# The input products of steps 4 to 7 of a residual LSTM: plain products replaced by two units of a seven-product scheme

## The chip, the core and the metric

The kernel runs on one core of one Trainium2 chip. The metric is the device time of one execution, in microseconds; where several runs stand together, their median is given. A core has five engines that each take their own instructions strictly in the order in which the program lists them: TensorE (PE in the profile; PEld is its weight loads), VectorE (DVE), ScalarE (ACT), GpSimd (POOL) and SyncE (SP). Here SyncE only issues transfers, and the others meet through semaphores.

## The reference, cut to what matters

An LSTM runs over 512 steps for 32 sequences with 512 inputs and 512 hidden units, in float32, and its outputs are added to its inputs.

```python
def lstm_forward(x, h0, Wx, Wh, b):           # x: 32 x 512 x 512, Wx and Wh: 512 x 2048
    xW = jnp.einsum('ntd,dg->ntg', x, Wx) + b # all steps, no recurrence
    def step(carry, xw_t):
        prev_h, prev_c = carry
        a = xw_t + prev_h @ Wh
        i, f, o = (sigmoid(a[:, k * Hd:(k + 1) * Hd]) for k in range(3))
        g = jnp.tanh(a[:, 3 * Hd:])
        next_c = f * prev_c + i * g
        return (o * jnp.tanh(next_c), next_c), o * jnp.tanh(next_c)
    ...
return x + lstm_forward(x, cond_1024, Wx, Wh, b)
```

`prev_h @ Wh` must be done step by step. `xW` has no recurrence, so its products can be done ahead and with fewer multiplications.

## The kernel before, in words

**Tiling.** A matmul of the kernel has 128 rows of contraction, 32 stationary columns (the 32 sequences of one step, or 32 rows of the state) and 256, 384, 128 or 512 moving columns. Four such matmuls, one for each quarter of the array's columns, run beside each other. Eight steps of `x` make a row (`ROW`); row 0 holds steps 0 to 7. The gate columns are cut in four blocks `j` of 512 (`NJ`), and the contraction in four quarters `q`. The weights `Wx` lie in SBUF as eight tiles `raw_sb`/`raw[i]`.

**Three ways to the input products.** (1) Plain (`direct`): 16 matmuls of 512 columns for a step. (2) A one-level unit: a 2 by 2 block scheme with seven products in place of eight, for one row and one block `j`. Its left sides are blocks of `x` or sums of them (`inner_sums`, the tiles `s_h`), its right sides are weights or differences of weights (`t_sums`, the tiles `t`). A unit needs seven product groups; each is eight matmuls of 256 columns, four for either half `k` of the contraction. (3) From row 4 on, two-level schemes (`PAIR`, `CYCLE`) whose right sides, the factors, are made once by VectorE (`push_factors`, tiles `wa_make` and `wb_make`), written to DRAM (`keep`) and streamed back.

**Windows.** Everything of ways 2 and 3 is paced by windows `v`. A unit that begins in window `v` has product group 1 and 5 in `v`, 6 in `v+1`, 7 in `v+2`, 2 and 3 in `v+3`, 4 in `v+4` (`products`). Between the windows' groups other engines must work (`evacuate`): ScalarE copies the accumulator `acc` after group 1 (`pu`) and group 5's bank `p`; VectorE adds `acc` and the copy of `p` after group 6 (into `pu`, called the pu add below: L617 before, L619 after) and again after group 7 (into `pp`, the pp add: L624 before, L626 after). Group 7 is added into the same half of `acc` that the pu add reads, so it waits for that add. One tile `acc` is one PSUM bank with two halves, and unit `n+2` has the other half of unit `n`'s tile; the program lets group 6 of unit `n+2` wait for the pp add of unit `n`.

**Order.** The program is written in one order by hand; each engine runs its share of it. VectorE's factor work is queued in `due` and let in by `run_due` within a room of columns: up to 1200 at a window's start, up to 1300 before the pp add, and up to 2400 more in a window that lies ahead of step 0. The operations of a window stand on VectorE's queue in just that order, so a pu add or pp add stands behind the factor work let in ahead of it.

**Ahead of step 0.** Steps 0 to 3 are done plainly while the weights arrive, into the four banks `firsts`, and kept by VectorE with the bias (`keep_direct`). Then window 0 (unit (1, 0)) and windows 1 to 4: each has one plain step (4 to 7) into a bank of `gates` and, up to window 3, the groups of the units of row 1. The first `PAIR_ROW - 1` rows after row 0 are done by units (`UNITS`), one a window. From step 0 on, step `k` runs with window `k + NJ`: 32 matmuls of the state (`h_part`, L851), the window's groups, and the cell.

**After a unit.** ScalarE copies its two result tiles, SyncE stores them to DRAM (`store`), and a later GpSimd transfer that adds (`load_xw`) brings a step's part into `xw`, which ScalarE has filled with the bias (`fill_bias`). Steps 0 to 7 take their `xw` straight from `keep_direct` instead.

Of the kernel before, what the change touches and what calls it, by code (L numbers as in the profile page):

```python
# [9 lines left out]
F32 = mybir.dt.float32  # L10
# [4 lines left out]
P = 128  # L15
B = 32
T = 512
NJ = 4
G = 4
IFG = 3 * P  # L20
ROW = 8
NROWS = T // ROW
C = 256
# [40 lines left out]
SLACK = [2, 2, 2, 8]  # L64
PAIR_SLACK = [2, 6]
AHEAD = 5
FACTORS_TO = 15

RAW_FIRST = 4

# [15 lines left out]

ROWS_AT = rows_by_use()
PAIR_ROW = 4
UNITS = [(i, j) for i in range(1, PAIR_ROW) for j in range(NJ)]

# [68 lines left out]


PAIR_STEP = 9
PAIR_AT = PAIR_STEP + NJ
PAIRS = len(PAIR_A_OF)
START = PAIR_AT + PAIRS
START_STEP = HEAD - LEAD
# [3 lines left out]
def windows_of(k):  # L171

    if k < PAIR_STEP:
        return [k + NJ]
    if k >= START_STEP:
        return [k + OFF]
    steps = START_STEP - PAIR_STEP
    lo, hi = (PAIRS * (k + e - PAIR_STEP) // steps for e in (0, 1))
    return list(range(PAIR_AT + lo, PAIR_AT + hi))
# [102 lines left out]
def kernel(  # L282
# [281 lines left out]
    def product(job, s, part=None):  # L564
        dst = {
            1: job.acc,
            6: job.acc,
            7: job.acc,
            5: p5[:, 0],
            2: job.pp[0][:, 0],  # L570
            3: job.pp[0][:, 1],
            4: job.pp[1][:, 0],
        }[s]
        for m, (a, w) in enumerate(job.factors(s)):
            if part not in (None, m):
                continue
            for t in range(4):
                nc.tensor.matmul(  # L578
                    dst[t * B : (t + 1) * B],
                    a[:, t],  # L580
                    w,
                    start=s in (1, 5) and m == 0,
                    stop=True,
                    skip_group_check=True,
                )
# [55 lines left out]
    def store(i, j, f):  # L641
# [3 lines left out]
        for t in range(4):  # L645
            nc.sync.dma_start(out=to[t, j * B : (j + 1) * B], in_=f[t * B : (t + 1) * B])

    def finish_unit(job, i, j, pool=unit_free):
        def finish(half):
            if half == 0:  # L650
                job.f = pool.pop(0)
            nc.scalar.copy(job.f[:, half], job.pp[half].rearrange("p n c -> p (n c)"))
            if half:
                store(i, j, job.f)
                pool.append(job.f)
            return 0

        return finish
# [113 lines left out]
    def keep_direct(t, bank, room=None):  # L772
        if room is not None:
            xw[t] = room
        elif t < 4:
            xw[t] = upool.tile([P, G * P], F32, name=f"xw_{t}", tag="xw", bufs=4)
        else:
            xw[t] = node_free[t - 4].rearrange("p t e b -> p (t e b)")
        nc.vector.tensor_add(xw[t], flat(bank), bias_sb)  # L779

    pieces = [(t, q, e) for t in range(LATE_END, T) for q in range(NJ) for e in (slice(0, C), slice(C, 2 * C))]
# [189 lines left out]
    for w, j in zip(LATE_AT, LATE_ORDER):  # L971
        job = new_job(w, True)
        job.kind = (None, j)
        job.acc, job.pp = jobs[LATE_AT[0]].acc, jobs[LATE_AT[0]].pp
    head_sums = {}

    def prepare(v):

        job = jobs.get(v)
        ops = []  # L980
        if job is None or job.w >= PAIR_AT:
            return ops
        i, j = job.kind
        for k in range(2):
            if (i, k) not in head_sums:
                if (i, 0) not in head_sums:
                    both = spool.tile([P, 2, 4, 4, B], F32, name=f"s_h{i}", tag="sums", bufs=2)
                head_sums[i, k], more = inner_sums(block(raw_block(i, k)), both[:, k])
                ops += more
        job.factors = lambda s: [  # L990
            (left(block(raw_block(i, k)), s, head_sums[i, k]), raw_factor(NJ * k + j, s)) for k in range(2)
        ]
        job.finish = finish_unit(job, i, j)
        job.release = lambda: None
        return ops
# [78 lines left out]
    def fetch(v):  # L1074

        job = jobs.get(v + 2)
        if job and LATE_AT[0] > job.w >= PAIR_AT and job.kept:
            job.ring = [rpool.tile([P, 3, C], F32, name=f"wa_{job.w}", tag="wa", bufs=3), None]
            nc.sync.dma_start(out=job.ring[0].rearrange("p n c -> p (n c)"), in_=job.kept[0])
        job = jobs.get(v)  # L1080
        if job and LATE_AT[0] > job.w >= PAIR_AT and job.kept:
            job.ring[1] = rpool.tile([P, 4, C], F32, name=f"wb_{job.w}", tag="wb", bufs=4)
            nc.sync.dma_start(out=job.ring[1].rearrange("p n c -> p (n c)"), in_=job.kept[1])
        if v in (LAST - 4, LAST - 2):
            load_row(END // ROW + (v - LAST + 4) // 2)
        for i in [i for i in range(8) if i not in RESIDENT][2 * (v - LAST) - 2 : 2 * (v - LAST)] if v > LAST else ():
            if i in again:
                f = free.pop(0)
                raw[i] = f.rearrange("p h (n c) -> p (h n) c", c=C)
            else:  # L1090
                raw[i] = rpool.tile([P, 4, C], F32, name=f"raw_again_{i}", tag="wb", bufs=4)
            nc.sync.dma_start(out=raw[i].rearrange("p n c -> p (n c)"), in_=wx[i])
        sb, rest = divmod(v + 8 - START, PER)
        if v + 6 in UNIT_AT[2 * NJ :: NJ]:
            load_row(3 + UNIT_AT[2 * NJ :: NJ].index(v + 6))
        if v in (NJ, NJ + 1):
            load_row(PAIR_ROW + v - NJ)
        if rest < MO and 0 <= sb < NSB:
            load_row(HEAD // ROW + MO * sb + ROWS_AT[rest])

    with tc.manual_schedule():
        warm = work.tile([P, G, P], F32, name="warm", tag="s")
        nc.scalar.activation(warm[:, 0], c_init, AF.Sigmoid)
        for m in range(10):
            nc.tensor.matmul(
                pps[2][m % NJ * B : (m % NJ + 1) * B].rearrange("p n c -> p (n c)"),
                c_init[:, 0:B],
                c_init.unsqueeze(1).to_broadcast([P, 4, P]),
                start=True,
                stop=True,  # L1110
            )
        nc.vector.transpose(
            bias_sb.rearrange("p (m l) -> p m l", l=B),
            bias_t.unsqueeze(2).to_broadcast([P, G * NJ, B]),
        )
        firsts = [gates[0], gates[1], pps[0], pps[1]]
        for q in range(4):
            for n in range(2):
                for t in range(4):
                    direct(t, firsts[t], (q,), slice(n * C, (n + 1) * C))  # L1120
        for i in range(5):
            for op in t_sums(i):
                op()
        keep_direct(0, firsts[0])
        for op in prepare(0):
            op()
        products(0)
        for t in range(1, 4):
            keep_direct(t, firsts[t])
        for i in range(5, 8):  # L1130
            for op in t_sums(i):
                op()
        push_factors()
        for v, t in enumerate(range(4, ROW), 1):
            direct(t, gates[t % 2])
            for op in prepare(v):
                op()
            if v < 4:
                evacuate(v, 0)
            run_due(0, 2400 if v > 1 else 0)  # L1140
            keep_direct(t, gates[t % 2])
            if v < 4:
                products(v)
                fetch(v)
        node_free[:] = node_free[NJ:] + node_free[:NJ]
        seed_first(0)
        seed_last(0)
        seed_first(1)

        for k in range(T):  # L1150
            if k % 2 == 0 and k + 2 < T:
                load_residual(k + 2)
            if 5 <= k and k + 3 < LATE_END:
                load_xw(k + 3)
            (h_part if k < HALVES else h_halves)(k)
            for m, v in enumerate(windows_of(k)):
                if v == PAIR_AT + RAW_FIRST - 1:
                    assert factors_left[-1] == 0
                if v == PAIR_AT + 4:
                    head_done()  # L1160
                announce(v)
                room = HEAD_ROOM if v < START - 4 else ROOM if k < HALVES - 1 else HALF_ROOM
                run_due(v, room - evacuate(v, room))
                products(v)
                tail_products(v)
                fetch(v)
                if m == 0:
                    if k == T - 2:
                        x_last()
                    if NJ <= k and k + 4 < LATE_END:  # L1170
                        fill_bias(k + 4)
                    (cell if k < HALVES else cell_halves)(k)
                    seed_first(k + 2)
                    seed_last(k + 1)
                for op in prepare(v + 1):
                    op()
        assert not due
# [51 lines left out]
```

## Time and profile before

| what | value |
|---|---|
| median of 3 runs (lowest to highest) | 3080.84 us (3080.80 to 3081.36) |
| the profiled execution's own time | 3080.69 us |
| its span, first to last instruction | 3078.9 us |
| TensorE busy | 3071.3 us |
| VectorE, ScalarE, GpSimd busy | 2284.0, 1975.9, 808.2 us |
| moved by DMA | 706.25 MB |

The span is what lies between the first and the last instruction; 1.79 us of the execution's own time lie outside it. Times in the timeline are counted from the span's start. In the records a matmul of this kernel stands as two, so a product group of eight stands as a row of x16. A row of the timeline gives start and duration; the duration of a pipelined instruction reaches into the next, so what one instruction costs its engine is read from start to start. Step 0's state products begin at 46.9 us.

### The profile page before, as it was taken

What the parts mean: (1) busy time and instruction counts of PE and PEld (TensorE: products, weight loads), DVE (VectorE), ACT (ScalarE), POOL (GpSimd) and SP (SyncE); (2) the same over time, 40 slices, a digit from 0 to 9 for tenths busy, and PEclk for the clock granted to TensorE, in tenths of its full rate; (3) what the DMA queues carried; (4) which work ended last, traced back from release to release, by engine and by line L of the source; (5) the groups of instructions that cost most, each with busy time, mean ns of one, the idle gap of its engine ahead of it and who ended that gap; (6) DMA issues with size and microseconds to landing.
All of it is one profiled execution on the core that took longest, in us unless ns stands there. A gap on an engine that the chain in (4) does not pass through costs nothing.

```text
span 3078.9 us, 133769 instructions
## 1 busy us (share of the span) xinstructions
PE 3071.3 (100%) x56644; PEld 1980.1 (64%) x56644; DVE 2284.0 (74%) x6437; ACT 1975.9 (64%) x5708; POOL 808.2 (26%) x1009
## 2 busy tenths in 40 slices
PE   9999999999999999999999999999999999999999
PEld 5555555556666666666666666666666666666666
DVE  6766777777777777777777777777777777777754
ACT  2566666666666666666666666766666666666664
POOL 0122222222222222222222222222222222222321
PEclk9999999999999999999999999999999999999999
DMA  9898898888889888898988988889898898988751
GB/s 318 239 260 214 228 258 220 250 224 239 245 212 263 229 239 239 213 265 211 259 224 216 265 224 249 226 222 261 215 261 227 227 255 218 258 226 222 194 118 41
DMA packets 349431, 706.25 MB, mean 229 GB/s; under 512 B 45600, under 2 KB 118688, under 8 KB 348320
## 3 DMA queue, kind: packets, MB, share of 16 engines
q1 hardware_dynamic: 276976, 567.36, 56.0%
q0 software_dynamic: 71424, 130.06, 26.4%
q8 instruction: 446, 7.31, 1.0%
q14 instruction: 153, 1.25, 0.1%
q10 hardware_dynamic: 432, 0.27, 0.0%
HBM read 512.83 MB, written 184.68 MB: 227 GB/s over the span
## 4 chain that ended last, share of the span: by engine, by line
PE 99%; DMA 0%; DVE 0%; ACT 0%; issue 0%; SPq 0%; DVEq 0%
PE gates L851 53%; PE acc L578 17%; PE pp L578 17%; PE p L578 6%; PE gates L865 4%; PE gates L763 1%; PE pp L763 1%; PE acc L763 0%; DMA raw_sb<-in_L_cond_Wx_dram 0%; ACT s L910 0%; DVE fc L916 0%; DVE c L918 0%; DVE fc L922 0%; DVE ig L917 0%; ACT ig L931 0%
## 5 line engine op out<-in xcount | busy, mean ns | idle before, releaser
L851 PE MATMUL gates<-wh_sb,ht 128*32 128x384 f32 (+1 forms) x30144 | 1723.1, 379 | 0.0
L851 PEld LDWEIGHTS gates<-wh_sb,ht 128*32 128x32 f32 x30144 | 1022.7, 110 | 704.5 <-issue 624.0
L954 POOL TENSOR_TENSOR oc<-xr,ht 128x128 f32<-128x128 f32 x509 | 386.3, 759 | 2232.2 <-DVE ht L896 2041.5
L813 POOL DMA_DIRECT2D xw<-xw x496 | 437.0, 881 | 21.4 <-ACT ig L931 2.4
L888 ACT ACTIVATE s<-gates 128x256 f32<-128x256 f32 x472 | 182.3, 386 | 343.4 <-PE gates L851 332.7
L809 ACT COPY xw<-bias_sb 128x512 f32<-128x512 f32 x496 | 313.4, 632 | 0.0
L578 PE MATMUL pp<-wb,nodes 128*32 128x256 f32 x3920 | 312.3, 379 | 0.0
L891 DVE TENSOR_TENSOR fc<-s,c 128x128 f32<-128x128 f32 x471 | 136.8, 290 | 184.4 <-ACT s L888 181.7
L622 ACT COPY pp<-pu 128x512 f32<-128x512 f32 x394 | 237.1, 602 | 53.0 <-DVE t L721 25.9
L895 DVE TENSOR_TENSOR fc<-s,ig 128x128 f32<-128x128 f32 x472 | 137.9, 292 | 177.3 <-ACT ig L894 177.3
L624 DVE TENSOR_TENSOR pp<-acc,p 128x256 f32<-128x256 f32 x394 | 168.4, 427 | 118.2 <-ACT pp L623 118.2
L890 ACT ACTIVATE s<-gates 128x128 f32<-128x128 f32 x472 | 131.4, 278 | 146.9 <-PE gates L851 146.7
L836 ACT COPY gates<-xw 128x384 f32<-128x384 f32 x468 | 221.2, 473 | 5.3 <-DVE nodes L779 5.3
L578 PE MATMUL acc<-wb,s 128*32 128x256 f32 x2656 | 211.5, 379 | 0.0
L578 PE MATMUL pp<-wb,s 128*32 128x256 f32 x2656 | 211.5, 379 | 0.0
L578 PE MATMUL acc<-wa,s 128*32 128x256 f32 x2656 | 211.5, 379 | 0.0
L578 PE MATMUL p<-wa,s 128*32 128x256 f32 x2656 | 211.4, 379 | 0.0
L894 ACT ACTIVATE ig<-c 128x128 f32<-128x128 f32 x472 | 146.3, 310 | 100.9 <-DVE c L893 62.8
L623 ACT COPY pp<-acc 128x256 f32<-128x256 f32 x394 | 142.2, 361 | 90.9 <-DVE t L721 41.1
L617 DVE TENSOR_TENSOR pu<-acc,p 128x256 f32<-128x256 f32 x394 | 163.8, 416 | 44.2 <-ACT p L614 35.4
L896 DVE STREAM_TRANSPOSE ht<-fc 128x128 f32<-128x128 f32 x472 | 147.0, 311 | 50.4 <-DVE fc L895 1.4
L614 ACT COPY p<-p 128x256 f32<-128x256 f32 x394 | 149.6, 380 | 39.8 <-PE p L578 37.7
(224 smaller groups left out, 4493.2 us busy)
## 6 DMA issues: line engine op xcount, KB each, us to landing
wb<-keep_b SPq DMA_DIRECT2D x332, 512.0 KB, 6.2
wa<-keep_a SPq DMA_DIRECT2D x332, 384.0 KB, 5.3
xw<-xw POOLq DMA_DIRECT2D x496, 256.0 KB, 5.7
xw<-t SPq DMA_DIRECT2D x420, 128.0 KB, 3.9
xw<-raw_sb SPq DMA_DIRECT2D x264, 128.0 KB, 3.9
xr<-in_x_dram SPq DMA_DIRECT2D x256, 128.0 KB, 5.5
out_dram<-oc SPq DMA_DIRECT2D x255, 128.0 KB, 4.6
row<-in_x_dram SPq DMA_DIRECT2D x63, 512.0 KB, 8.3
```

Source lines behind the costliest of these rows:

```text
L578: nc.tensor.matmul(dst[t * B : (t + 1) * B], a[:, t], w, start=s in (1, 5) and m == 0, stop=True, skip_group_check=True,)
L614: nc.scalar.copy(job.p5, p5[:, 0])
L617: nc.vector.tensor_add(job.pu[:, 1], job.acc, job.p5)
L622: nc.scalar.copy(job.pp[0], job.pu)
L624: nc.vector.tensor_add(job.pp[1][:, 1], job.acc, job.p5)
L809: nc.scalar.copy(xw[t], bias_sb)
L813: nc.gpsimd.dma_start(out=xw[t], in_=stored[i][a], accum_op=mybir.AluOpType.add)
L836: nc.scalar.copy(gates[t % 2][:, 0:IFG], xw[t][:, 0:IFG])
L851: nc.tensor.matmul(g[j * B : (j + 1) * B, cols], state["ht"][:, k, :], wh_sb[:, k, j, cols], start=False, stop=True, skip_group_check=True,)
L888: nc.scalar.activation(s[:, 0:2], g[:, 0:2], AF.Sigmoid)
L896: nc.vector.transpose(ht.rearrange("p q b -> p (q b)"), h)
L954: (nc.gpsimd if t < T - 3 else nc.vector).tensor_add(state["oc"][:, tt % 2], xr[t][:, tt % 2], ht)
```

## The change

Steps 4 to 7 are no longer done plainly. Two units are put ahead of the others: each has the four steps 4 to 7 (half a row, `h = 1`) and two column blocks, `js = (0, 1)` and `(2, 3)`, where a unit of the other kind has eight steps and one column block. Its groups have as many matmuls as those of the others; the left sides have 64 columns for each half of the contraction in place of 128, and both new units share one set of left sums, kept in a tile of `nodes`. Six units (two new, four of row 1) now stand in windows 0 to 5, ahead of step 0, one after the other; step `k` runs with window `k + 6`, so it meets the same unit as before. The results of steps 4 to 7 go through DRAM as those of later steps do. One weight tile's differences (`t_sums(5)`) are made ahead of window 0 and not behind it. `FACTORS_TO`, the window by which all factors must be made, goes from 15 to 17.

```diff
-FACTORS_TO = 15
+FACTORS_TO = 17
...
-UNITS = [(i, j) for i in range(1, PAIR_ROW) for j in range(NJ)]
+UNITS = [(0, (1, (0, 1))), (0, (1, (2, 3)))] + [(i, j) for i in range(1, PAIR_ROW) for j in range(NJ)]
+FIRST = 2 + NJ
...
-                    a[:, t],
-                    w,
+                    a[:, t % a.shape[1]],
+                    w[t // a.shape[1]] if isinstance(w, list) else w,
...
+    def half_block(src, h):
+
+        return lambda g, e: src[:, 4 * h + 2 * g : 4 * h + 2 * g + 2, e]
+
+    def half_factors(i, h, js, made):
+        return lambda s: [
+            (left(half_block(raw_block(i, k), h), s, made[k]), [raw_factor(NJ * k + j, s) for j in js])
+            for k in range(2)
+        ]
...
-        for i in range(5):
+        for i in range(6):
             for op in t_sums(i):
                 op()
         keep_direct(0, firsts[0])
         for op in prepare(0):
             op()
         products(0)
         for t in range(1, 4):
             keep_direct(t, firsts[t])
-        for i in range(5, 8):
+        for i in range(6, 8):
             for op in t_sums(i):
                 op()
         push_factors()
-        for v, t in enumerate(range(4, ROW), 1):
-            direct(t, gates[t % 2])
+        for v in range(1, FIRST):
             for op in prepare(v):
                 op()
-            if v < 4:
-                evacuate(v, 0)
+            evacuate(v, 0)
             run_due(0, 2400 if v > 1 else 0)
-            keep_direct(t, gates[t % 2])
-            if v < 4:
-                products(v)
-                fetch(v)
-        node_free[:] = node_free[NJ:] + node_free[:NJ]
+            products(v)
+            fetch(v)
+        for op in prepare(FIRST):
+            op()
+        run_due(0, 2400)
...
-            if 5 <= k and k + 3 < LATE_END:
+            if 1 <= k and k + 3 < LATE_END:
                 load_xw(k + 3)
...
-                    if NJ <= k and k + 4 < LATE_END:
+                    if k + 4 < LATE_END:
                         fill_bias(k + 4)
```

Three places show how the instructions move. First TensorE, from group 5 of the second unit to group 1 of the third (`p` is group 5's bank, `acc` the accumulators, `s_h` and `nodes` the left sums). Before:

```order
L578 MATMUL p_85<-t_95,s_h_341 32x256 x4
L578 MATMUL p_85<-t_99,s_h_341 32x256 x4
L763 MATMUL gates_82<-raw_sb,row_102 32x512 x16
L578 MATMUL acc_83<-t_94,s_h_341 32x256 x4
L578 MATMUL acc_83<-t_98,s_h_341 32x256 x4
L578 MATMUL acc_83<-raw_sb,row_117 32x256 x8
```

And with the change:

```order
L580 MATMUL p_85<-t_96,nodes_174 32x256 x2
L580 MATMUL p_85<-t_97,nodes_174 32x256 x2
L580 MATMUL p_85<-t_100,nodes_174 32x256 x2
L580 MATMUL p_85<-t_101,nodes_174 32x256 x2
L580 MATMUL acc_83<-t_94,nodes_174 32x256 x2
L580 MATMUL acc_83<-t_95,nodes_174 32x256 x2
L580 MATMUL acc_83<-t_98,nodes_174 32x256 x2
L580 MATMUL acc_83<-t_99,nodes_174 32x256 x2
L580 MATMUL acc_83<-raw_sb,row_117 32x256 x8
```

The plain step between group 5 of the second unit and group 7 of the first is gone; the two groups stand directly behind each other.

Second VectorE, from the end of the last weight differences (`t_101`) to the first pu add. Before:

```order
L368 TENSOR_TENSOR t_101<-raw_sb,t_101 128x256
L417 TENSOR_TENSOR wa_make_405<-raw_sb 128x256
L779 TENSOR_TENSOR nodes_174<-gates_81,bias_sb 128x512
L417 TENSOR_TENSOR wa_make_405<-raw_sb 128x512
L617 TENSOR_TENSOR pu_408<-acc_83,p_0_410 128x256
```

And with the change:

```order
L370 TENSOR_TENSOR t_101<-raw_sb,t_101 128x256
L419 TENSOR_TENSOR wa_make_388<-raw_sb 128x256
L447 TENSOR_TENSOR s_h_419<-row_117 128x128
L448 TENSOR_TENSOR s_h_419<-s_h_419,row_117 128x128
L449 TENSOR_TENSOR s_h_419<-row_117 128x128
L450 TENSOR_TENSOR s_h_419<-row_117,s_h_419 128x128
L447 TENSOR_TENSOR s_h_419<-row_117 128x128
L448 TENSOR_TENSOR s_h_419<-s_h_419,row_117 128x128
L449 TENSOR_TENSOR s_h_419<-row_117 128x128
L450 TENSOR_TENSOR s_h_419<-row_117,s_h_419 128x128
L419 TENSOR_TENSOR wa_make_388<-raw_sb 128x512
L619 TENSOR_TENSOR pu_391<-acc_83,p_0_393 128x256
```

The keeping of a plain step is gone from this place, and the eight left sums of row 1, which stood ahead of window 0 before, now stand ahead of the first pu add.

Third VectorE again, from the second pu add to the first pp add. Before:

```order
L617 TENSOR_TENSOR pu_454<-acc_84,p_1_456 128x256
L417 TENSOR_TENSOR wb_make_465<-t_97,t_94 128x1024
L417 TENSOR_TENSOR wa_make_529<-raw_sb 128x256
L417 TENSOR_TENSOR wa_make_529<-raw_sb 128x512
L417 TENSOR_TENSOR wb_make_530<-t_98,t_100 128x1024
L417 TENSOR_TENSOR wa_make_538<-raw_sb 128x256
L624 TENSOR_TENSOR pp_87<-acc_83,p_0_410 128x256
```

And with the change:

```order
L619 TENSOR_TENSOR pu_429<-acc_84,p_1_431 128x256
L419 TENSOR_TENSOR wb_make_440<-t_97,t_94 128x1024
L419 TENSOR_TENSOR wa_make_485<-raw_sb 128x256
L419 TENSOR_TENSOR wa_make_485<-raw_sb 128x512
L419 TENSOR_TENSOR wb_make_486<-t_98,t_100 128x1024
L626 TENSOR_TENSOR pp_87<-acc_83,p_0_393 128x256
```

The same factor work stands between the two adds but for one piece of 256 columns, which now comes behind the pp add.

More of the change, by code (lines that the diff above doesn't have):

```diff
@@ L163 @@
 PAIR_STEP = 9
-PAIR_AT = PAIR_STEP + NJ
+PAIR_AT = PAIR_STEP + FIRST
 PAIRS = len(PAIR_A_OF)
@@ L173, in windows_of @@
     if k < PAIR_STEP:
-        return [k + NJ]
+        return [k + FIRST]
     if k >= START_STEP:
@@ L646, in store, with store_half @@
             nc.sync.dma_start(out=to[t, j * B : (j + 1) * B], in_=f[t * B : (t + 1) * B])
+    def store_half(i, h, js, f):
+        if i not in stored:
+            stored[i] = dram.tile([ROW, P, 2 * C], F32, name=f"xw_{i}", tag="xw", bufs=8)
+        to = stored[i].rearrange("(u g t) p c -> u t p g c", u=2, g=2)
+        for at, j in enumerate(js):
+            for t in range(2):
+                lo = (2 * at + t) * B
+                nc.sync.dma_start(out=to[h, t, j * B : (j + 1) * B], in_=f[lo : lo + B])
+    def half_block(src, h):
[5 more added lines that the diff above has]
+        ]
     def finish_unit(job, i, j, pool=unit_free):
@@ L653, in finish @@
             if half:
-                store(i, j, job.f)
+                if isinstance(j, tuple):
+                    store_half(i, *j, job.f)
+                else:
+                    store(i, j, job.f)
                 pool.append(job.f)
@@ L774, in keep_direct @@
             xw[t] = room
-        elif t < 4:
+        else:
             xw[t] = upool.tile([P, G * P], F32, name=f"xw_{t}", tag="xw", bufs=4)
-        else:
-            xw[t] = node_free[t - 4].rearrange("p t e b -> p (t e b)")
         nc.vector.tensor_add(xw[t], flat(bank), bias_sb)
@@ L975 @@
     head_sums = {}
+    half_sums, half_room = [], []
     def prepare(v):
@@ L983, in prepare @@
         i, j = job.kind
+        if isinstance(j, tuple):
+            h, js = j
+            if not half_sums:
+                half_room.append(node_free.pop(0))
+                both = half_room[0].rearrange("p (k g t) e b -> p k g (t e) b", k=2, g=4)
+                for k in range(2):
+                    made, more = inner_sums(half_block(raw_block(i, k), h), both[:, k])
+                    half_sums.append(made)
+                    ops += more
+            job.factors = half_factors(i, h, js, half_sums)
+            job.finish = finish_unit(job, i, j)
+            job.release = lambda: None
+            return ops
         for k in range(2):
@@ L1093, in fetch @@
         sb, rest = divmod(v + 8 - START, PER)
[L1094 to L1097, printed above, removed]
+        if v == UNIT_AT[UNITS.index((3, 0))] - 6:
+            load_row(3)
+        if v in (FIRST, FIRST + 1):
+            load_row(PAIR_ROW + v - FIRST)
         if rest < MO and 0 <= sb < NSB:
@@ L1158 @@
                     assert factors_left[-1] == 0
+                if v == FIRST + 4:
+                    node_free.extend(half_room)
                 if v == PAIR_AT + 4:
```

## The prediction

> **What bounds the kernel now.** I read the page first: busy times and the chain that ended last.
>
> ```profile
> PE 3071.3 (100%) x56644; PEld 1980.1 (64%) x56644; DVE 2284.0 (74%) x6437; ACT 1975.9 (64%) x5708; POOL 808.2 (26%) x1009
> PE 99%; DMA 0%; DVE 0%; ACT 0%; issue 0%; SPq 0%; DVEq 0%
> ```
>
> TensorE is busy all the way, and the chain is TensorE from end to end. So the time changes by what the change adds to or takes from TensorE's own work, and by every wait it brings where there was none. The averages don't say how near other engines are in the stretch that is rewritten; the busy times by stretch do:
>
> ```profile
> 20.00:45.00 25.00, 25.00 (x360) 11.57 (x356) 22.59 (x49) 3.48 (x9) 0.00 (x0) 1.00 1.02 381
> 45.00:100.00 55.00, 55.00 (x1004) 31.50 (x1000) 35.98 (x82) 26.84 (x76) 5.63 (x7) 1.00 0.75 244
> ```
>
> After the length come PE, PEld, DVE, ACT and POOL. Between 20 and 45 us, just the stretch of the plain steps and first units, VectorE is busy for 22.59 us of 25 and TensorE never waits; from 45 us on VectorE has a third of its time free. Before step 0, then, VectorE is the second bound, and the order there decides. So I read the timeline of both engines from 17 to 47 us. TensorE:
>
> ```profile
> 20.23 1.05 PE L578 MATMUL acc<-raw_sb,row 128*32 128x256 f32 x16
> 21.09 1.05 PE L578 MATMUL p<-t,s_h 128*32 128x256 f32 x16
> 21.95 3.62 PE L763 MATMUL gates<-raw_sb,row 128*32 128x512 f32 x32
> 25.39 1.05 PE L578 MATMUL acc<-raw_sb,row 128*32 128x256 f32 x16
> ...
> 33.14 1.05 PE L578 MATMUL acc<-t,s_h 128*32 128x256 f32 x16
> ...
> 46.91 3.64 PE L851 MATMUL gates<-wh_sb,h_init 128*32 128x384 f32 x64
> ```
>
> Start to start a product group costs 0.86 us and a plain step 3.44 us, four groups' worth. Step 0 starts at 46.91.
>
> **The change part by part.** *TensorE's own work.* Four plain steps go (4 x 3.44 = 13.76 us), two units of seven groups come (14 x 0.86 = 12.04 us): -1.7 us. That is all that can be gained, since the rest of the kernel keeps its matmuls.
>
> *What the plain steps also did* is to keep TensorE busy for 3.44 us in each window while ScalarE and VectorE served the units. To price the loss I walk VectorE's queue as the order of the change gives it, with the starts of the same instructions in the trace:
>
> ```profile
> 17.61 0.69 DVE L366 TENSOR_TENSOR t<-raw_sb 128x512 f32<-128x512 f32 x1 [0.42 <-DMA raw_sb<-in_L_cond_Wx_dram]
> ...
> 19.18 0.69 DVE L779 TENSOR_TENSOR xw<-gates,bias_sb 128x512 f32<-128x512 f32 x1
> 19.79 0.28 DVE L445 TENSOR_TENSOR s_h<-row 128x128 f32<-128x128 f32 x1
> ...
> 21.66 0.68 DVE L779 TENSOR_TENSOR xw<-gates,bias_sb 128x512 f32<-128x512 f32 x1
> ...
> 23.45 0.68 DVE L366 TENSOR_TENSOR t<-raw_sb 128x512 f32<-128x512 f32 x1
> ...
> 24.97 0.68 DVE L366 TENSOR_TENSOR t<-raw_sb 128x512 f32<-128x512 f32 x1
> ...
> 28.01 0.42 DVE L417 TENSOR_TENSOR wa_make<-raw_sb 128x256 f32<-128x256 f32 x1
> 28.34 0.68 DVE L779 TENSOR_TENSOR nodes<-gates,bias_sb 128x512 f32<-128x512 f32 x1
> 28.94 0.68 DVE L417 TENSOR_TENSOR wa_make<-raw_sb 128x512 f32<-128x512 f32 x1
> 29.54 0.42 DVE L617 TENSOR_TENSOR pu<-acc,p 128x256 f32<-128x256 f32 x1
> ```
>
> Each piece is the distance between two of these starts: one keeping 0.61 (19.18 to 19.79), eight left sums 1.87 (to 21.66), three keepings 1.79 (to 23.45), one tile of weight differences 1.52 (to 24.97), a factor piece of 256 columns 0.33, one of 512 columns 0.60. The new half sums have 64 columns; the trace has 64-column operations near its end:
>
> ```profile
> 2880.49 0.23 DVE L916 TENSOR_TENSOR fc<-s,c 128x64 f32<-128x64 f32 x1 [1.32 <-ACT s L910]
> 2880.63 0.22 DVE L917 TENSOR_TENSOR ig<-s 128x64 f32<-128x64 f32 x1
> 2880.88 0.23 DVE L918 TENSOR_TENSOR c<-fc,ig 128x64 f32<-128x64 f32 x1
> ```
>
> 0.14 us each, 0.25 where one reads the one before; four sums with one such step 0.67, eight 1.34.
>
> *First wait.* Up to 19.18 VectorE does what it did, set by the weights' arrival (17.61). Then, in the new order: `t_sums(5)` 1.52, keeping 0.61, half sums 1.34, three keepings 1.79, `t_sums(6)` and `(7)` 3.04, factor piece 0.33, the eight sums of row 1 1.87, factor piece 0.60: the pu add begins at 19.18 + 11.10 = 30.28 and ends 0.42 later, at 30.70. Group 7 of the first unit waits for it. What a wait for VectorE costs beyond the record's end is seen near the end of the trace:
>
> ```profile
> 3070.12 0.18 DVE L916 TENSOR_TENSOR fc<-s,c 128x64 f32<-128x64 f32 x1
> ...
> 3070.34 0.81 PE L865 MATMUL gates<-wh_sb,ht 128*32 128x256 f32 x9 [1.17 <-DVE fc L916]
> ```
>
> 0.04 us. So group 7 starts at 30.74. Ahead of it TensorE has only five groups now (1, 5 | 1, 6, 5): unhindered 20.23 + 5 x 0.86 = 24.53. It waits 6.2 us in all. A part of that falls earlier, on the half sums (21.5) and on the weight differences of tiles 6 and 7 (26.6), but the sum is set by the pu add. Before, two plain steps (6.88 us) stood in this place and VectorE had the pu add out at 29.54.
>
> *Second wait.* From 30.74 TensorE has six groups, to 35.90: 7, 1, 6, 5, 7, 1. The next, group 6 of the third unit, waits for the first unit's pp add. VectorE's part begins with the second pu add, which waits for TensorE's third group of these six (end 33.32):
>
> ```profile
> 34.32 0.42 DVE L617 TENSOR_TENSOR pu<-acc,p 128x256 f32<-128x256 f32 x1 [1.37 <-PE acc L578]
> 34.66 1.22 DVE L417 TENSOR_TENSOR wb_make<-t,t 128x1024 f32<-128x1024 f32 x1
> 35.79 1.02 DVE L417 TENSOR_TENSOR wa_make<-raw_sb 128x256 f32<-128x256 f32 x2
> 36.73 1.22 DVE L417 TENSOR_TENSOR wb_make<-t,t 128x1024 f32<-128x1024 f32 x1
> 38.41 0.43 DVE L417 TENSOR_TENSOR wa_make<-raw_sb 128x256 f32<-128x256 f32 x1 [0.46 <-DMA keep_b<-wa_make]
> ```
>
> The group whose end released it began at 33.14 and so ended at 34.00; the add began 0.32 later. Then pu add 0.34, factor pieces 1.13, 0.94 and 1.13: the pp add starts 3.54 after the pu add. Now: 33.32 + 0.32 + 3.54 = 37.18, and 0.43 + 0.04 later TensorE goes on, at 37.65 in place of 35.90: 1.75 us. Before, a plain step stood in this window too.
>
> *Later windows.* From the third on, ScalarE's copies lead to the pp add:
>
> ```profile
> 48.61 0.58 ACT L652 COPY slot<-pp 128x512 f32<-128x512 f32 x1
> ...
> 50.53 0.43 DVE L624 TENSOR_TENSOR pp<-acc,p 128x256 f32<-128x256 f32 x1 [1.42 <-ACT pp L623]
> ```
>
> 1.92 from the first copy to the add, 0.47 for the add, and 0.25 to 0.32 from a group's end to the copy: 2.64 to 2.71, while TensorE has three groups (2.58). So 0.06 to 0.13 in each of the two windows left, about 0.1 to 0.3; I take 0.1. VectorE's wait for a write of a factor (38.41, 0.46) comes here too, but the next add that TensorE needs has two groups of room behind it; if the writes come 2 us later, that room is gone and 0.5 to 1 us is added.
>
> *What else moves.* ScalarE gets 16 copies, VectorE 12 additions and sums for 4 keepings, SyncE 8 stores, GpSimd 4 adding transfers, all off TensorE's path once the windows again hold 32 state matmuls. Two windows' more factor work is done ahead of step 0, so less is left behind it; TensorE had no wait there to lose, so nothing is gained. Steps 4 to 7 now depend on a store and an adding transfer:
>
> ```profile
> xw<-xw POOLq DMA_DIRECT2D x496, 256.0 KB, 5.7
> xw<-t SPq DMA_DIRECT2D x420, 128.0 KB, 3.9
> ```
>
> The last half unit's copy goes out in step 0's window; 3.9 + 5.7 = 9.6 us later the first input is there, while step 4's gates are filled after step 2's cell, over 20 us later. Price nothing; if that cover went, ScalarE would stand still and each late step would show.
>
> *The sum.* 6.2 + 1.75 + 0.1 - 1.7 = +6.3 us. Against the profiled execution, 3080.69 + 6.3 = 3087.0; against the median 3080.84, 3087.1. I forecast 3087.0, its own range 3086.2 to 3087.9: hops of 0.02 to 0.1 us on some ten waits, the later windows, 2% on VectorE's pieces.
>
> **The rivals.** *(1) Only the first wait is paid: not slower by over 0.2%.* Place: group 6 of the third unit. If the factor pieces ahead of the pp add were done by the time the six groups end (5.16 us after the pu add), the second wait is nil: 6.2 - 1.7 = +4.5, 3085.2. For it: it is a difference of two near sums (4.33 against 2.58 us after the third group). Against it: the pieces stand in the order one by one, and each has its duration above. It decides if the chain is shorter by 1.75.
>
> *(2) The clock.* With these waits TensorE does only two of a group's eight matmuls now and then between about 24.8 and 30.7 us. The opening and the end show what idleness does:
>
> ```profile
> 1.06 4.94 PE L1105 MATMUL pp<-c_init 128*32 128x512 f32 x20 [1.06 <-DVE c_init L349]
> 3060.00:3079.00 19.00, 12.61 (x228) 8.54 (x224) 8.43 (x40) 6.04 (x30) 0.46 (x1) 0.96 0.06 16
> 3070.34 2.83 PE gates L865 x48
> ```
>
> The first 20 records of 512 columns took 4.94 us, 247 ns each, against 3.44/32 = 108 ns in the plain steps: less than half speed for the first 4.9 us. At the end the granted clock averages 0.96 over 19 us, that is half clock for the last 1.5 us, from 3077.5 on, 4.3 us after the last matmuls (3073.2). So an idle stretch of at most 4.3 us lowers the clock, and up to 4.9 us then run at half speed: +2.5 us, 3089.5. Against it: the longest whole standstill that I count is 3.9 us (26.8 to 30.7), a little under 4.3, broken by two matmuls before. The Trainium skill (TensorE: Matmul & The Clock Gate, Part 1: The HAM clock gate) says that the clock halves after one idle window of about 3.4 us, that these windows run freely, and that one busy window restores it. By that rule an estimate of the loss is 3.4/2 = 1.7 us, 3088.7, in only those executions whose window falls inside the standstill.
>
> *(3) The run keeps pace after all:* the group order hides both waits, only -1.7 stays, 3079.0. For it speaks nothing but that I may misread what a group waits for.
>
> *(4) An input of steps 4 to 7 comes late:* one adding transfer of 5.7 us shows, 3092.7. The margin above speaks against it.
>
> **How the numbers follow.** About 0.2%, 6.2 us or a time of 3087.0, is what a measurement of this kernel can tell from no change. Chances: forecast 0.56, rival 1 0.14, clock 0.24, keeping pace 0.04, late input 0.02. The forecast's own range lies across 3087.0: I count 0.33 of it above, 0.23 below, a little more above since the small terms left out only add. Slower 0.33 + 0.24 + 0.02 = 0.59; same 0.23 + 0.14 + 0.03 = 0.40; faster 0.01, if more than the TensorE work is saved. The range 3085.5 to 3089.6 holds the forecast, the clock and the upper part of rival 1.
>
> **What would show it.** In the profile of the changed kernel: TensorE's slices ahead of step 0 no longer full; two waits for VectorE, L619 at about 30.7 (the pieces up to it 6.2 us in all) and L626 at about 37.6 (1.7 us); step 0's state products at 46.9 + 6.3 = 53.2; and from there the distance to the kernel before unchanged to the end. If step 0 starts at 51.4, rival 1 holds; at 45.2, rival 3. Matmuls at over 200 ns a record of 512 columns, or a granted clock under 1.00 between 28 and 36 us, would be rival 2. A distance that grows between steps 2 and 7 would be rival 4. The forecast is wrong if TensorE waits for something else there, or if the waits come out under 6.5 us in all.

## The result, and the profile after

The change makes the kernel slower: 3089.18 us (3088.61 to 3089.74, 10 runs) against 3080.91 us (3080.76 to 3081.36, 10 runs), a ratio of 1.0027, 95% interval 1.0018 to 1.0035. That is 8.3 us more; 3087.0 was forecast, 3085.5 to 3089.6 the range. The median lies near the upper end of that range and outside the forecast's own (3086.2 to 3087.9); four of the ten executions took more than 3089.6. The profiled execution took 3089.66 us, so it is one of the slower ones; its span is 3087.9.

The page still shows TensorE busy all the way, but the first slice of the second row, which was a 9 before, is no longer full, and VectorE has a share of the chain:

```profile
PE 3073.6 (100%) x56740; PEld 1964.9 (64%) x56740; DVE 2284.7 (74%) x6445; ACT 1982.0 (64%) x5724; POOL 810.2 (26%) x1013
PE   8999999999999999999999999999999999999999
PE 99%; DVE 1%; DMA 0%; SPq 0%; issue 0%; ACT 0%; DVEq 0%
```

Busy time went up by 2.3 us, though TensorE got less work (96 more records, but of 256 columns where those that went had 512): matmuls ran slower somewhere. TensorE's waits for VectorE (total, times, longest):

```profile
PE acc L580 <- DVE pu L619: 3.4, 1, 3.4
PE acc L580 <- DVE pp L626: 1.6, 1, 1.6
...
PE p L580 <- DVE t L368: 0.9, 1, 0.9
PE p L580 <- DVE nodes L447: 0.5, 1, 0.5
```

These are the two waits that were foretold, L619 and L626, and the two small ones ahead of the first. TensorE's timeline of the stretch:

```profile
20.23 1.05 PE L580 MATMUL acc<-raw_sb,row 128*32 128x256 f32 x16
...
24.59 1.37 PE L580 MATMUL p<-t,nodes 128*32 128x256 f32 x12
26.86 0.63 PE L580 MATMUL p<-t,nodes 128*32 128x256 f32 x4 [0.90 <-DVE t L368]
30.91 1.94 PE L580 MATMUL acc<-t,nodes 128*32 128x256 f32 x16 [3.43 <-DVE pu L619]
32.62 1.93 PE L580 MATMUL acc<-raw_sb,row 128*32 128x256 f32 x16
34.33 1.70 PE L580 MATMUL acc<-t,nodes 128*32 128x256 f32 x16
35.86 1.04 PE L580 MATMUL p<-t,s_h 128*32 128x256 f32 x16
36.72 1.04 PE L580 MATMUL acc<-t,nodes 128*32 128x256 f32 x16
37.59 1.04 PE L580 MATMUL acc<-raw_sb,row 128*32 128x256 f32 x16
40.21 1.07 PE L580 MATMUL acc<-t,s_h 128*32 128x256 f32 x16 [1.58 <-DVE pp L626]
...
56.11 3.64 PE L873 MATMUL gates<-wh_sb,h_init 128*32 128x384 f32 x64
```

Group 7 of the first unit starts at 30.91 (30.74 foretold). Then three groups cost 1.71, 1.71 and 1.53 us from start to start, and only the fourth 0.86 again: 4.95 us for what takes 2.59 at full speed. The granted clock, the share of full speed at which TensorE may run, is the third figure from the end in these rows, and it says why:

```profile
28.00:29.00 1.00, 0.00 (x0) 0.00 (x0) 0.96 (x6) 0.00 (x0) 0.00 (x0) 0.92 1.04 401
29.00:32.00 3.00, 1.08 (x12) 0.59 (x16) 2.97 (x8) 0.00 (x0) 0.00 (x0) 0.50 1.04 395
32.00:35.00 3.00, 3.00 (x32) 1.38 (x28) 0.93 (x2) 0.37 (x1) 0.00 (x0) 0.50 1.06 401
35.00:36.00 1.00, 1.00 (x16) 0.47 (x12) 0.00 (x0) 0.00 (x0) 0.00 (x0) 0.67 1.06 404
```

An average of 0.92 over a microsecond is half clock for its last 0.16 us, one of 0.67 half clock for its first 0.66 us: from 28.84 to 35.66 TensorE ran at half clock, 6.8 us. It fell while TensorE waited and was not back for the first three groups. This is the second rival. VectorE's side shows that the queue itself went as walked:

```profile
17.82 0.69 DVE L368 TENSOR_TENSOR t<-raw_sb 128x512 f32<-128x512 f32 x1 [0.61 <-DMA raw_sb<-in_L_cond_Wx_dram]
...
29.84 0.69 DVE L419 TENSOR_TENSOR wa_make<-raw_sb 128x512 f32<-128x512 f32 x1
30.44 0.42 DVE L619 TENSOR_TENSOR pu<-acc,p 128x256 f32<-128x256 f32 x1
...
36.18 0.42 DVE L619 TENSOR_TENSOR pu<-acc,p 128x256 f32<-128x256 f32 x1 [3.25 <-PE acc L580]
...
39.73 0.42 DVE L626 TENSOR_TENSOR pp<-acc,p 128x256 f32<-128x256 f32 x1
```

The weights came 0.21 us later than in the profile before (17.82 against 17.61), the pu add began at 30.44 (30.28 foretold), and from the second pu add to the pp add it took 3.55 us (3.54).

From step 0 on nothing more is added. The chain has the state products of step 4 and of a step near the end, before:

```profile
85.08 3.45 PE gates L851 x64
3060.33 3.66 PE gates L865 x64
```

And with the change:

```profile
94.28 3.45 PE gates L873 x64
3069.42 3.54 PE gates L887 x64
```

They are 9.20 and 9.09 us apart; the distance is 9.20 at step 0 and at each of the ten steps behind it. The inputs of steps 4 to 7 through DRAM cost nothing.

### The profile page after: what moved, and what is told of

It reads as the page before. It is cut to its first block, busy times and chain, and to the rows that moved or that the text cites. A ratio compares the mean times of both kernels' runs of the same rounds, so it can differ in the third digit from the quotient of the medians.

```text
span 3087.9 us, 134012 instructions
## 1 busy us (share of the span) xinstructions
PE 3073.6 (100%) x56740; PEld 1964.9 (64%) x56740; DVE 2284.7 (74%) x6445; ACT 1982.0 (64%) x5724; POOL 810.2 (26%) x1013
## 4 chain that ended last, share of the span: by engine, by line
PE 99%; DVE 1%; DMA 0%; SPq 0%; issue 0%; ACT 0%; DVEq 0%
PE gates L873 53%; PE pp L580 17%; PE acc L580 17%; PE p L580 6%; PE gates L887 4%; PE acc L787 0%; PE pp L787 0%; DMA raw_sb<-in_L_cond_Wx_dram 0%; SPq L342 0%; DVE t L368 0%; DVE xw L801 0%; DVE wb_make L419 0%; DVE t L369 0%; DVE t L370 0%; DVE wa_make L419 0%
## 5 line engine op out<-in xcount | busy, mean ns | idle before, releaser
L626 DVE TENSOR_TENSOR pp<-acc,p 128x256 f32<-128x256 f32 x396 | 169.2, 427 | 131.9 <-ACT pp L625 131.9
L619 DVE TENSOR_TENSOR pu<-acc,p 128x256 f32<-128x256 f32 x396 | 164.6, 416 | 43.6 <-ACT p L616 35.7
```

The costliest lines, as they stand in the source:

```text
L619: nc.vector.tensor_add(job.pu[:, 1], job.acc, job.p5)
L626: nc.vector.tensor_add(job.pp[1][:, 1], job.acc, job.p5)
```

## The experiments

The theory after the result: VectorE's queue makes TensorE wait about 8 us ahead of step 0, and because TensorE then does next to nothing for 6 us, the clock halves and costs about 2 us more. The rival: the queue alone sets the time, the slow matmuls lie under waits that would be there anyway.

**e1: the first wait filled.** A plain step's matmuls go into the wait; their result is used by nothing.

```diff
             products(v)
+            if v == 1:
+                direct(4, gates[0])
             fetch(v)
```

> One plain step's matmuls (16 of 512 columns, 3.44 us, their result used by nothing) put into the first wait, between group 5 of the second unit and group 7 of the first. Theory (queue and clock: VectorE's queue makes TensorE wait 8 us ahead of step 0, and the near standstill from 24.8 to 30.9 us then halves the clock up to 35.7 us): the matmuls fit into the wait, the granted clock stays 1.00, TensorE's next groups take 0.86 us each, step 0 at about 53.5 us, time about 3087.2 (3086.8 to 3087.8). Rival (the queue alone, the clock costs nothing by itself since VectorE sets the pace): no change, about 3089.2.

Measured: 3087.6 us (3087.05 to 3088.39), against 3081.08 before; 1.0022, interval 1.0013 to 1.0031. All 10 executions had a mean granted clock of 1.000, where all 10 of the change had 0.999. TensorE's rows:

```profile
27.61 3.60 PE L787 MATMUL gates<-raw_sb,row 128*32 128x512 f32 x30
31.21 1.07 PE L580 MATMUL acc<-t,nodes 128*32 128x256 f32 x16
32.10 1.05 PE L580 MATMUL acc<-raw_sb,row 128*32 128x256 f32 x16
...
38.17 1.07 PE L580 MATMUL acc<-t,s_h 128*32 128x256 f32 x16 [1.57 <-DVE pp L626]
```

The 16 more matmuls fit into the wait, the groups behind it cost 0.86 to 0.89 us, and the second wait is as long as with the change (1.57 for 1.58). More work on TensorE made the kernel 1.75 us faster, taking each against the kernel before that it ran with (8.27 and 6.52 us more), and its slowest execution (3088.39) lies under the fastest with the change (3088.61): that is the clock's share. The rival, which expected 3089.2, falls. What is left, 6.5 us, is the forecast without the clock (6.3).

**e2: factor work put off.** No factor work on VectorE before window 4.

```diff
-            push(2 + (FACTORS_TO - 2) * i // len(ops), columns, go, lambda _, i=i: len(done) == i)
+            push(5 + (FACTORS_TO - 5) * i // len(ops), columns, go, lambda _, i=i: len(done) == i)
...
-        taken = run_due(v - 0.5, FIRST_SUMS)
+        taken = run_due(v - 0.5, FIRST_SUMS if v > 3 else 0)
...
-            run_due(0, 2400 if v > 1 else 0)
+            run_due(0, 2400 if v > 3 else 0)
```

> No factor work on VectorE before window 4 (the rooms of windows 1 to 3 are nil, the due windows begin at 5 and not at 2). Theory (queue and clock): the first pu add comes 0.93 us earlier (two factor pieces gone ahead of it), the second wait goes to about 0.2 us; the near standstill is still over 5 us, so the clock still falls: about 3089.2 - 0.9 - 1.5 = 3086.8. Rival 1 (only the first wait is real): 3088.3. Rival 2 (factor work put off comes back as waits later): 3089 or more.

Measured: 3086.54 us (3085.32 to 3088.17); 1.0019, interval 1.0010 to 1.0028. The clock was 0.999 in nine executions of ten; the tenth, at 1.000, is the fastest.

```profile
29.79 1.07 PE L580 MATMUL acc<-t,nodes 128*32 128x256 f32 x16 [2.49 <-DVE pu L619]
30.67 1.88 PE L580 MATMUL acc<-raw_sb,row 128*32 128x256 f32 x16
32.30 1.95 PE L580 MATMUL acc<-t,nodes 128*32 128x256 f32 x16
34.01 1.12 PE L580 MATMUL p<-t,s_h 128*32 128x256 f32 x16
...
35.81 1.05 PE L580 MATMUL acc<-raw_sb,row 128*32 128x256 f32 x16
36.86 1.07 PE L580 MATMUL acc<-t,s_h 128*32 128x256 f32 x16
...
30.00:31.00 1.00, 1.00 (x20) 0.53 (x16) 0.00 (x0) 0.00 (x0) 0.00 (x0) 0.87 1.05 406
```

The first wait is 0.94 us shorter by the profile (2.49 for 3.43), the second is down to 0.2 (36.67 to 36.86), and the clock still falls: the last row is one by stretch, and its 0.87 is half clock from 30.74 on. So both waits are real, both come from what stands ahead of the adds on VectorE's queue, and the factor work put off is not missed later: the distance to the kernel before is 5.85 us at step 0 (52.76 against 46.91) and 5.94 near the end (3061.09 against 3055.15).

**e3: the sums of row 1 behind the first pu add**, on top of e2.

```diff
-            for op in prepare(v):
-                op()
+            made = prepare(v)
+            if v != 2:
+                for op in made:
+                    op()
             evacuate(v, 0)
+            if v == 2:
+                for op in made:
+                    op()
```

> As e2, and the eight left sums of row 1 stand behind the first pu add. Theory (queue and clock): the pu add is another 1.87 us earlier, group 7 starts at about 27.9 us; between 24.8 and 27.9 us TensorE is near idle for 3.1 us only, under a clock window of 3.4 us, so the clock holds in all or most executions: waits 3.4 us in all, 3080.9 - 1.7 + 3.4 + 0.3 = 3082.9, step 0 at about 48.9. Rival (no clock loss, then none to win back): 3086.8 - 1.9 = 3084.9.

Measured: 3083.09 us (3082.56 to 3085.12); 1.0007, interval 0.9998 to 1.0016. Eight executions had a clock of 1.000 and took 3082.56 to 3083.31, two had 0.999 and took 3085.05 and 3085.12. One and the same kernel thus shows the price of a fall of the clock, 2.1 us between the middles, and the rival, which expected 3084.9, falls. The wait for the pu add is short now, and step 0 stands 0.7 us behind the place expected (48.9):

```profile
28.30 1.07 PE L580 MATMUL acc<-t,nodes 128*32 128x256 f32 x16 [0.63 <-DVE pu L619]
...
49.59 3.64 PE L873 MATMUL gates<-wh_sb,h_init 128*32 128x384 f32 x64
```

**e4: the adds first.** On top of e3, the four keepings of steps 0 to 3 and the last two operations of `t_sums(7)` stand behind the first pu add; two of the keepings stand ahead of the first pp add, the other two behind it. The last piece below is in `evacuate`, ahead of the pp add.

```diff
-        keep_direct(0, firsts[0])
+        rooms += [upool.tile([P, G * P], F32, name=f"xw_{t}", tag="xw", bufs=4) for t in range(4)]
         for op in prepare(0):
             op()
         products(0)
-        for t in range(1, 4):
-            keep_direct(t, firsts[t])
-        for i in range(6, 8):
-            for op in t_sums(i):
-                op()
+        for op in t_sums(6):
+            op()
+        last_tile = t_sums(7)
+        last_tile.pop(0)()
...
             if v == 2:
-                for op in made:
+                for op in last_tile + made:
                     op()
+            if v == 3:
+                for t in (0, 1):
+                    keep_direct(t, firsts[t], rooms[t])
...
+            if v == 3:
+                for t in (2, 3):
+                    keep_direct(t, firsts[t], rooms[t])
```

> As e3, and the four keepings of steps 0 to 3 and the last two operations of t_sums(7) stand behind the adds that TensorE waits for. Theory (queue and clock): waits of about 0.4 us are left, the 1.7 us of TensorE's own work are gained: 3080.9 - 1.7 + 0.4 = 3079.6, step 0 at about 45.6. Rival (the units cost something besides VectorE's queue, such as the inputs of steps 4 to 7 through DRAM, or the factor work put off): 3081 or more, with step 0 at 45.6 and the distance growing later.

Measured: 3079.91 us (3079.41 to 3080.46, 11 runs) against 3081.08 us before (3080.71 to 3081.47, 33 runs): 1.2 us faster, and no execution of either lies in the other's range; the ratio's interval, 0.9997 with 0.9988 to 1.0005, does not set it apart from no change. The waits are gone, but for 0.15 to 0.3 us in each of three windows:

```profile
24.69 1.10 PE L580 MATMUL acc<-t,nodes 128*32 128x256 f32 x16
25.56 1.10 PE L580 MATMUL acc<-raw_sb,row 128*32 128x256 f32 x16
...
29.01 1.10 PE L580 MATMUL acc<-raw_sb,row 128*32 128x256 f32 x16
30.16 1.07 PE L580 MATMUL acc<-t,s_h 128*32 128x256 f32 x16
...
46.06 3.64 PE L877 MATMUL gates<-wh_sb,h_init 128*32 128x384 f32 x64
```

Group 7 of the first unit, at 30.91 with the change, starts at 24.69; step 0 at 46.06, 0.85 us ahead of the kernel before in this execution, the slowest of the eleven. So the whole loss is the order on VectorE's queue and what follows from it, and the units themselves do save TensorE's time. That the rest of the 1.7 us went into the small waits is worked out, not tried: by the rows up to step 0 they come to 0.75 us, and the first group starts 0.07 us later than with the change (20.30).

The lead of 0.85 us does not last in this execution: 0.56 us of it goes at 1075, where TensorE breaks off in a product group without a wait that the profile shows, and a step near the end starts at 3055.26 against 3055.15. The rival had a distance that grows later. The other ten executions, all faster, have no profile; their median, 1.2 us ahead, speaks against a loss that is always there, but what breaks TensorE off stays open.

**e5 and e6: how little work keeps the clock.** As e1 with a quarter and a half of the plain step.

```diff
-                direct(4, gates[0])
+                direct(4, gates[0], (0,))        # e5
+                direct(4, gates[0], (0, 1))      # e6
```

> As e1 with a quarter of the plain step put into the first wait: 4 matmuls of 512 columns, 0.86 us, in place of 16 and 3.44 us. The open point is how little work keeps the clock. Between 24.8 and 30.9 us TensorE then works 1.3 us in place of 0.4. If a clock window must be all but empty to count as idle (in the changed kernel one with 0.4 us of matmuls counted): the clock holds in all executions, the time is that of e1, about 3087.6, clock 1.000. If a share of busy time over about a third is asked for: the clock falls in most, about 3089.2, clock 0.999.

> As e5 with half of the plain step, 8 matmuls of 512 columns, 1.72 us. By either account nearer to e1: if the window must be all but empty, 3087.6 and clock 1.000 as in e5 and e1; if a share of over about a third is asked for, the clock falls in some executions only, median 3087.6 to 3089. If e5 and e6 both stay at 3089.2, it is the length of the standstill behind the filler (over 2 us) that counts and not the share.

Measured: e6 3087.42 us (3086.98 to 3088.61), the clock 1.000 in all ten executions. e5 3088.62 us (3087.19 to 3089.37): four executions at 1.000 took 3087.19 to 3087.63, six at 0.999 took 3088.57 to 3089.37. The first account, by which the clock holds in all executions of e5, falls. The second is near for e5 (it falls in most, six of ten), but it let the clock fall in some executions of e6, and it fell in none. Within e5 a fall costs 1.8 us between the middles. The profiled execution of e5 is one where it fell:

```profile
28.00:31.00 3.00, 0.60 (x6) 0.00 (x0) 2.93 (x11) 0.16 (x1) 0.00 (x0) 1.00 1.02 392
31.00:32.00 1.00, 0.83 (x16) 0.55 (x20) 1.00 (x2) 0.00 (x0) 0.00 (x0) 1.00 1.06 394
32.00:35.00 3.00, 3.00 (x36) 1.49 (x28) 1.18 (x3) 0.37 (x1) 0.00 (x0) 0.50 1.04 391
35.00:36.00 1.00, 1.00 (x20) 0.57 (x16) 0.21 (x1) 0.00 (x0) 0.00 (x0) 0.78 1.01 382
```

It fell at 32.0, when TensorE had been at work again for 0.8 us, and came back at 35.4. The half clock lasted 3.4 us here and 6.8 us, twice that, with the change, as if the clock were decided on stretches of 3.4 us. If the stretch that ended at 32.0 was as long, from 28.6 on, it had 0.83 us of matmuls, a quarter of its time, and still counted as idle; in e2 the stretch up to 30.74 would have had 0.95 us, from 29.79 on. That the stretch ends just at the fall is an assumption which no run tests by itself.

## Why the prediction was right, and where it was short

- **TensorE's own work, -1.7 us:** borne out by e4, where step 0 comes 0.85 us earlier and the small waits and the later start take the other 0.8; its median keeps 1.2 us.
- **First wait, 6.2 us:** from 24.53, where five groups would have ended, to 30.91: 6.4 us. The 0.17 us more is the later arrival of the weights, 0.21 us at 17.82.
- **Second wait, 1.75 us:** from 38.45 (37.59 and a group of 0.86) to 40.21, 1.76 us.
- **Later windows, 0.1 us:** mis-sized. The prediction's own working gave 0.1 to 0.3 us and took the least. The group that waits for a pp add stands 0.15 us late in either window by these rows, and 0.03 us more goes into the group after it, 0.3 to 0.4 us in all:

```profile
45.41 1.05 PE L580 MATMUL acc<-raw_sb,row 128*32 128x256 f32 x16
46.42 1.07 PE L580 MATMUL acc<-t,s_h 128*32 128x256 f32 x16
47.31 1.05 PE L580 MATMUL p<-t,s_h 128*32 128x256 f32 x16
...
51.62 1.05 PE L580 MATMUL acc<-raw_sb,row 128*32 128x256 f32 x16
52.63 1.07 PE L580 MATMUL acc<-t,s_h 128*32 128x256 f32 x16
```

- **The clock, put at a chance of 0.24:** it came in every execution, and this is the step that failed. The sign that was named for it, a granted clock under 1.00 between 28 and 36 us, is what the profile shows. The prediction held against it that the longest whole standstill, 3.9 us (3.43 by the row at 30.91), was under 4.3 us, with two matmuls before it. A whole standstill of that length was not needed: the clock fell at 28.84, when TensorE had stood still for 1.35 us (the row at 26.86 ends at 27.49), and in the 3.4 us before the fall six records had still begun, the last two of the row at 24.59 and the four at 26.86, 0.3 us of work at 0.054 us each. In the profiled execution it cost 4.95 - 2.59 = 2.4 us, in the median 1.75 (e1); 2.5 was the rival's price from the trace. The estimate by the rule of the Trainium skill (TensorE: Matmul & The Clock Gate, Part 1: The HAM clock gate) was 1.7 us, and its window of about 3.4 us that runs freely agrees with the trace, half clock for 3.4 us in e5 and 6.8 us with the change, and with e3 and e5, where one program falls in some executions only. Its word "idle" is wider than I read it.
- **Sum of the profiled execution:** 6.4 + 1.76 + 0.4 + 2.4 - 1.7 = 9.3 us, against 9.20 at step 0.
- **Rival 1** (the second wait is nil): fell, 1.76 us by the profile; e2 is the kernel in which that wait is nearly gone. **Rival 3** (the run keeps pace) needs the other order, e4. **Rival 4** (late inputs): fell, the distance stays.

So the direction and the mechanism of the two waits were right, and the likeliest number was 2.2 us short, 1.75 of it because the clock stood as a rival and not as a term. Without the clock, e1's 6.5 us more lie within 0.2 us of the forecast's 6.3. That the median fell into the range at all, 0.4 us under its upper end, is owed to the room that was left for the clock, not to the sum.

## What to carry to other kernels

Work that looks like overhead on the busiest engine can be the cover under which the next engine serves it: before taking it out, walk the queue of that next engine up to the operation the busy one will wait for, and put that operation ahead of everything that nobody waits for. Where the busiest engine is TensorE and it comes near a standstill for some 3 us (e3: the clock fell in two executions of ten) or 6 us (the change: in ten of ten), count the loss of the clock as a term of the sum and not as a mishap. Matmuls of no use, put into the wait, can be worth more than they cost (1.75 us in e1), though the right order is worth more still (9.4 us between the change and e4). A unit that saves arithmetic saves time only once its results are fetched in step.

## What the runs showed of the hardware

I had not expected that the clock falls though TensorE is back at work (e5: down at 32.0 after 0.83 us of work; e2: down at 30.74 after 0.95 us), so that a stretch of 3.4 us with a quarter of its time in matmuls seems to count as idle. In e2 the longest whole standstill was 2.49 us, and the clock fell in nine executions of ten. Nor had I expected that work only from 30.91 on did not bring the clock back at once (the change: half clock from 28.84 to 35.66; if these are two stretches of 3.4 us, the first, to 32.25, had 1.3 us of half-speed work). With 1.72 us of matmuls in the wait (e6) the clock held ten times of ten, with 0.86 us (e5) four times, with none (the change) never.
